# Row convolutions as six products for four pixels on whole images, shorter reciprocal roots, and new due times in a planned kernel

## The chip, the cores and the metric

The kernel runs on one core of one Trainium2 chip. The metric is device time in microseconds (us) of one execution, compared by the median of several. The engines have the profile's names: PE is TensorE (matmuls), PEld its weight loads, DVE is VectorE, ACT is ScalarE, POOL is GpSimd, SP is SyncE, which here only issues transfers.

## The reference

The input is `x`, eight images of 256 channels and 32 x 32 pixels in float32. Four layers follow, each added to its input. Each but for the last sees the input normalised in 32 groups of channels.

```python
x = x + _L0_conv_ref(_gn(x), ...)   # attention, 8 heads of 64, q and k scaled to length one
x = x + _L1_conv_ref(_gn(x), ...)   # 3x3 convolution 256 -> 256, weights times a scale per output channel
x = x + _L2_conv_ref(_gn(x), ...)   # 3x3 convolution 256 -> 256
x = x + _L3_conv_ref(_gn(x), ...)   # mixer: 4 branches of a selective scan, gate, three row filters,
                                    # attention with 8 heads of 32, gelu, 3x3 filter per channel, projection

def _gn(v, G=32, eps=1e-5):
    B_, C_, H_, W_ = v.shape
    g = v.reshape(B_, G, C_ // G, H_, W_)
    m = jnp.mean(g, axis=(2, 3, 4), keepdims=True)
    s = jnp.var(g, axis=(2, 3, 4), keepdims=True)
    return ((g - m) / jnp.sqrt(s + eps)).reshape(v.shape)

def _L2_conv_ref(inp, kernel, bias):
    out = lax.conv_general_dilated(inp, kernel, window_strides=(1, 1), padding=((1, 1), (1, 1)), ...)
    return out + bias[None, :, None, None]
```

The output is the last `x`. The change concerns the two 3x3 convolutions (layers 1 and 2), every reciprocal root of the normalisations, one small product of the mixer's gate, and the order of all work.

## The kernel before

Every operation is first recorded and then put in order by a planner inside the kernel, so that all instructions of the profile carry one line, L252, that of the recorder's call. `gather` joins neighbouring matmuls, `depend` finds what each must wait for, and `rank` gives each group a due time: the work belongs to streams, one per image and part, and the table `PACE` holds seven marks for each stream, between which the due times are laid by the share of the stream's work done. A due time is never earlier than that of what the operation depends on. `arrange` then simulates the engines with a small cost table and issues, on the engine that is free first, the ready group that can start first, by due time among equals. What results is one fixed order per engine. The marks decide nothing but this order.

The streams of an image are A (attention of layer 0), O (its projection), C (both convolutions), N (normalisations ahead of the mixer), F0 to F3 (front of each branch), S (the scans), Z0 to Z3 (end of each branch), B (gate, filters, attention of the mixer) and E (end). W and V prepare weights at the start. Several images are under way at once: while TensorE works at the attention of one image, VectorE runs the scans of another. Only one image can be in C at a time, since the tile `xt` of the pool `xp` has one buffer; so does the tile `taps`.

A convolution (`conv3x3`) works in halves of 16 rows. `transform` normalises the image into `taps` on ScalarE, odd and even pixels apart, and makes from them, for each pair of pixels of a row, four inputs: the row transform by which two outputs of a three-tap filter need four products in place of six. For each half, each block of 128 output channels (`m`) and each of two parts, twelve matmuls of 256 columns fill one PSUM tile `cv` (two buffers) with two products: six matmuls each, for three rows of the filter and two blocks of input channels. `add_products` then adds them on VectorE to the pixels in `xt`, which lie two floats apart. In layer 1 the scale per output channel is applied there, through `col("s1", m)` and `minus_s1`. The weights of the products are made once at the start by `conv_weights` in the tiles `room`, stored in DRAM (`made_w`, 12 pieces of 256 KB for each layer), and loaded by `chunk` from there, piece by piece through ScalarE's queue, for each half again.

`inverse_root` makes a reciprocal root in 11 small operations on VectorE: two for a first guess from the bits, and three Newton steps of three. Four callers use it: `group_stats`, the lengths of q and k, `layer_norm`, and the normalisation in `back_end`, 12 calls an image.

In `back_layers` the gate's 1-wide convolution is one matmul of 128 output columns for each of two blocks and two halves, with the weights spread out in `qpr`.

Of the kernel before, what the change touches and what calls it, by code (L numbers as in the profile page):

```python
# [12 lines left out]
F32 = mybir.dt.float32  # L13
I32 = mybir.dt.int32
AF = mybir.ActivationFunctionType
ALU = mybir.AluOpType
# [23 lines left out]
        (-1169, -859, -431, 125, 565, 748, 863),  # L40
        (2031, 2138, 2230, 2316, 2394, 2427, 2468),
        (3022, 3122, 3226, 3328, 3426, 3535, 3634),
        (4218, 4286, 4354, 4427, 4500, 4575, 4647),
        (5274, 5344, 5414, 5494, 5578, 5649, 5689),
        (6338, 6402, 6470, 6543, 6618, 6719, 6822),
        (7394, 7477, 7560, 7650, 7740, 7826, 7869),
        (8432, 8500, 8566, 8639, 8712, 8760, 8799),
    ),
    "B": (
        (3742, 3818, 3894, 3959, 4024, 4099, 4174),  # L50
        (4850, 4908, 4966, 5025, 5083, 5138, 5192),
        (5827, 5907, 5970, 6049, 6107, 6107, 6280),
        (6819, 6852, 6882, 7048, 7214, 7265, 7312),
        (7970, 8053, 8136, 8225, 8314, 8393, 8472),
        (9010, 9104, 9202, 9300, 9398, 9514, 9630),
        (10029, 10029, 10029, 10122, 10143, 10411, 10586),
        (12739, 12779, 12790, 12925, 12925, 12925, 12925),
    ),
    "C": (
        (1590, 1668, 1685, 1828, 1928, 1928, 1981),  # L60
        (1459, 2140, 2729, 2891, 3004, 3103, 3202),
        (3333, 3631, 3802, 3930, 4058, 4186, 4314),
        (4584, 4720, 4870, 4997, 5122, 5250, 5374),
        (5516, 5743, 5908, 6052, 6195, 6329, 6462),
        (6973, 7034, 7094, 7165, 7233, 7365, 7527),
        (7722, 7896, 8016, 8164, 8316, 8462, 8608),
        (8801, 8855, 9006, 9179, 9350, 9442, 9586),
    ),
    "E": (
        (4173, 4210, 4252, 4314, 4346, 4378, 4412),  # L70
        (5281, 5299, 5322, 5360, 5390, 5426, 5463),
        (6271, 6328, 6375, 6404, 6452, 6489, 6531),
        (7362, 7383, 7418, 7456, 7517, 7539, 7559),
        (8230, 8230, 8477, 8544, 8580, 8609, 8648),
        (9051, 9054, 9067, 9081, 9151, 9151, 9156),
        (10314, 10413, 10427, 10973, 11043, 11080, 11119),
        (10605, 10611, 10611, 10621, 10759, 10804, 10844),
    ),
    "F0": (
        (936, 936, 936, 992, 1236, 1236, 1289),  # L80
        (2142, 2142, 2375, 2438, 2500, 2699, 2699),
        (1749, 1791, 1821, 1868, 1868, 1967, 1995),
        (2036, 2036, 2127, 2174, 2174, 2174, 2174),
        (2752, 2933, 2957, 3038, 3038, 3176, 3176),
        (3833, 3833, 3833, 3880, 3880, 3883, 3883),
        (7322, 7383, 7488, 7535, 7637, 7778, 7778),
        (4815, 4875, 4875, 4922, 4993, 4993, 5007),
    ),
    "F1": (
        (2076, 2151, 2335, 2371, 2411, 2420, 2432),  # L90
        (3681, 3742, 3771, 3771, 3789, 3798, 3807),
        (4629, 4639, 4648, 4671, 4765, 4775, 4784),
        (5763, 5791, 5809, 5840, 5882, 5903, 5940),
        (6643, 6661, 6670, 6716, 6801, 6809, 6892),
        (7897, 7897, 7933, 7950, 7956, 7972, 7980),
        (8743, 8757, 8769, 8817, 8833, 8845, 8851),
        (9880, 9881, 9912, 10075, 10121, 10181, 10225),
    ),
    "F2": (
        (2483, 2632, 2659, 2683, 2686, 2696, 2724),  # L100
        (3391, 3605, 3653, 3712, 3782, 3828, 3866),
        (4779, 4809, 4840, 4849, 4849, 4938, 5017),
        (5860, 5870, 5879, 5899, 5942, 5952, 5965),
        (6960, 6979, 7003, 7004, 7005, 7061, 7143),
        (7482, 7818, 8051, 8054, 8055, 8139, 8147),
        (8917, 9009, 9012, 9027, 9046, 9065, 9128),
        (10350, 10379, 10379, 10492, 10492, 10492, 10492),
    ),
    "F3": (
        (2951, 2953, 2976, 2976, 2996, 2996, 3002),  # L110
        (4074, 4078, 4080, 4081, 4091, 4143, 4210),
        (5062, 5119, 5141, 5146, 5158, 5184, 5247),
        (6098, 6100, 6114, 6114, 6123, 6273, 6386),
        (7109, 7138, 7166, 7203, 7257, 7277, 7353),
        (8377, 8384, 8391, 8432, 8450, 8453, 8500),
        (9289, 9311, 9331, 9331, 9331, 9341, 9408),
        (10811, 10811, 10811, 10815, 10815, 10815, 10815),
    ),
    "N": (
        (-721, -721, -719, -694, -694, -375, -322),  # L120
        (792, 849, 849, 1025, 1763, 1835, 1835),
        (1854, 1854, 1854, 1854, 1854, 1897, 2131),
        (1094, 1117, 1128, 1226, 1226, 4468, 6014),
        (4191, 4193, 4193, 4350, 4350, 4677, 4847),
        (4700, 4700, 4700, 4700, 4700, 4813, 4838),
        (6559, 6654, 6654, 6654, 6654, 6732, 6732),
        (7299, 7299, 7299, 7313, 7313, 7314, 7695),
    ),
    "O": (
        (2052, 2052, 2092, 2101, 2104, 2104, 2109),  # L130
        (2440, 2440, 2442, 2506, 2528, 2619, 2658),
        (3608, 3632, 3649, 3701, 3731, 3752, 3770),
        (4659, 4659, 4704, 4704, 4704, 4704, 4704),
        (5731, 5762, 5778, 5800, 5800, 5811, 5815),
        (6790, 6818, 6831, 6831, 6853, 6853, 6855),
        (7980, 7995, 8002, 8007, 8007, 8012, 8019),
        (8777, 8905, 8909, 8909, 8909, 8919, 8921),
    ),
    "S": (
        (2406, 2724, 2768, 2976, 3146, 3269, 3410),  # L140
        (3494, 3698, 3902, 4034, 4182, 4361, 4540),
        (4529, 4737, 4950, 5093, 5238, 5409, 5573),
        (5564, 5777, 5988, 6129, 6269, 6446, 6622),
        (6667, 6869, 7053, 7214, 7359, 7529, 7696),
        (7697, 7932, 8138, 8275, 8411, 8578, 8763),
        (8777, 8978, 9185, 9338, 9524, 9669, 9853),
        (10860, 10860, 10860, 10869, 10880, 10900, 10900),
    ),
    "V": (
        (-528, -402, -399, 138, 415, 459, 459),  # L150
    ),
    "Z0": (
        (2585, 2611, 2631, 2682, 2705, 2755, 2761),
        (3563, 3649, 3649, 3649, 3649, 3896, 4005),
        (4787, 4787, 4827, 4831, 4878, 4924, 4965),
        (5794, 5794, 5806, 5980, 6230, 6230, 6230),
        (6835, 6842, 6868, 6877, 6877, 7018, 7030),
        (7547, 7547, 7628, 7960, 7983, 8769, 8891),
        (8907, 8957, 8998, 9005, 9013, 9291, 9316),
        (10109, 10118, 10158, 10340, 10340, 10345, 10490),  # L160
    ),
    "Z1": (
        (2375, 2417, 2433, 2705, 2793, 2846, 3222),
        (3815, 3815, 3815, 3845, 3936, 3965, 4022),
        (4921, 4945, 4958, 5048, 5091, 5103, 5133),
        (5915, 5953, 5970, 5970, 6079, 6085, 6088),
        (7089, 7093, 7093, 7095, 7097, 7101, 7135),
        (8059, 8083, 8108, 8113, 8113, 8113, 8363),
# [2209 lines left out]
```

## Time and profile before

| | |
|---|---|
| median of 3 runs | 5131.74 us (5129.71 to 5144.03) |
| the profiled execution | 5126.34 us, its span 5124.6 us |
| TensorE matmul | 4740.6 us busy, 93% of the span, 19178 records |
| VectorE | 4040.2 us busy, 79%, 5586 instructions |
| ScalarE | 2908.5 us busy, 57%, 3829 instructions |
| mean granted clock of TensorE | 0.957 |
| convolution matmuls (`cv<-taps,w`) | 737.5 us busy, 3072 records |
| transfers | 575.20 MB, of them `w<-wc` 384 times 256 KB |

Each float32 matmul leaves two records of weight load and two of matmul. Matmuls of less than 128 rows or columns can run beside each other; the busy time of an engine is the time in which at least one of its instructions runs, and a mean duration of a group can contain overlap with its neighbours. The granted clock is the share of TensorE's full clock that was granted.

### The profile page before, as it was taken

How to read it: one execution, taken by the hardware profiler on the slowest of the kernel's cores; microseconds unless marked ns; L12 is line 12 of the kernel's file. 1: busy time of each engine (PE TensorE's matmuls, PEld its weight loads, DVE VectorE, ACT ScalarE, POOL GpSimd, SP SyncE). 2: the span in 40 equal slices, each digit the busy share in tenths (PEclk: the TensorE clock that was granted, in tenths of full speed). 3: DMA queues.
4: the chain of work that ended last, by engine and by line, in shares of the span. 5: the costliest groups of instructions: out<-in, count | busy, mean ns of one | idle time of the engine just before them, and what ended most of it. 6: DMA issues, size and time to landing. Idle time of an engine off the chain costs nothing.

```text
span 5124.6 us, 53905 instructions
## 1 busy us (share of the span) xinstructions
PE 4740.6 (93%) x19178; PEld 1940.5 (38%) x19178; DVE 4040.2 (79%) x5586; ACT 2908.5 (57%) x3829; POOL 17.8 (0%) x26
## 2 busy tenths in 40 slices
PE   8999799999999999999999999998999899888796
PEld 3362253253432534243442344325343343422323
DVE  4336989996988967988797998788778899799802
ACT  4426545556665565656566566555656557566352
POOL 0000000000000000000000000000000000000000
PEclk9999999999999999999999999999999999899897
DMA  4133253343333433433433353325333344334200
GB/s 135 46 124 113 98 171 120 100 153 116 116 113 102 136 104 113 121 108 125 130 95 104 114 169 112 106 69 162 117 97 112 124 140 152 95 125 125 81 23 25
DMA packets 256662, 575.20 MB, mean 112 GB/s; under 512 B 51192, under 2 KB 79224, under 8 KB 256384
## 3 DMA queue, kind: packets, MB, share of 16 engines
q1 hardware_dynamic: 167680, 431.11, 26.9%
q10 hardware_dynamic: 88704, 140.55, 8.9%
q8 instruction: 154, 2.52, 0.2%
q14 instruction: 124, 1.02, 0.1%
HBM read 483.18 MB, written 63.18 MB: 107 GB/s over the span
## 4 chain that ended last, share of the span: by engine, by line
PE 64%; DVE 24%; ACT 6%; issue 3%; DMA 3%; SPq 1%; DVEq 0%; ACTq 0%
PE big L252 36%; PE cv L252 14%; DVE hs L252 14%; PE acc L252 11%; PE y L252 3%; ACT p L252 2%; DVE room L252 1%; DVE st L252 1%; DVE p L252 1%; DVE u L252 1%; DVE xt L252 1%; DVE xm L252 1%; SPq L252 1%; DVE taps L252 1%; ACT taps L252 1%
## 5 line engine op out<-in xcount | busy, mean ns | idle before, releaser
L252 ACT ACTIVATE p<-big 128x1024 f32<-128x1024 f32 x1024 | 1013.9, 1019 | 555.0 <-PE big L252 489.0
L252 ACT ACTIVATE da<-dt,a_neg 128x512 f32<-128x512 f32 x1024 | 728.1, 720 | 609.2 <-DVE hs L252 494.4
L252 PE MATMUL acc<-p,v 128*64 128x512 f32 x3072 | 833.1, 624 | 41.7 <-ACT p L252 37.4
L252 PE MATMUL cv<-taps,w 128*128 128x256 f32 x3072 | 737.5, 391 | 26.9 <-DVE taps L252 20.7
L252 PEld LDWEIGHTS cv<-taps,w 128*128 128x128 f32 x3072 | 580.0, 193 | 264.7 <-issue 137.0
L252 DVE TENSOR_TENSOR hs<-du,bc 128x1024 f32<-128x1024 f32 x512 | 615.3, 1213 | 64.8 <-PE y L252 55.8
L252 DVE TENSOR_TENSOR hs<-hs,bc 128x1024 f32<-128x1024 f32 x512 | 623.8, 1218 | 31.8 <-ACT carry L252 30.3
L252 DVE TENSOR_TENSOR_SCAN hs<-da,carry,hs 128x512 f32<-128x512 f32 x512 | 637.6, 1273 | 2.1 <-ACT da L252 1.8
L252 PE MATMUL big<-q,k 64*128 64x512 f32 x2048 | 586.7, 652 | 36.4 <-ACT p L252 25.9
L252 DVE TENSOR_TENSOR_SCAN hs<-da,hs 128x512 f32<-128x512 f32 x512 | 608.9, 1213 | 5.6 <-ACT da L252 3.8
L252 DVE TENSOR_TENSOR p<-p 128x1024 f32<-128x1024 f32 x256 | 312.2, 1220 | 205.5 <-ACT p L252 125.9
L252 PEld LDWEIGHTS acc<-p,v 128*64 128x64 f32 x3072 | 161.8, 136 | 603.0 <-issue 416.0
L252 PE MATMUL y<-hs,sel 128*32 128x512 f32 x2048 | 318.5, 632 | 69.6 <-DVE hs L252 61.8
L252 PEld LDWEIGHTS big<-q,k 64*128 64x128 f32 x2048 | 160.9, 188 | 432.6 <-issue 210.8
L252 PE MATMUL big<-qk,qk 32*128 32x512 f32 x2048 | 303.4, 645 | 5.6 <-ACT qk L252 1.6
L252 PE MATMUL cv<-p,v 128*64 128x512 f32 x1024 | 279.1, 612 | 0.0
L252 PE MATMUL big<-xn,w 128*128 128x512 f32 x512 | 236.3, 608 | 6.7 <-ACT big L252 4.1
L252 PE MATMUL big<-o,w 128*128 128x512 f32 x384 | 178.6, 608 | 5.3 <-DVE o L252 2.0
L252 PE MATMUL big<-room,w 128*128 128x512 f32 (+3 forms) x308 | 149.5, 640 | 29.2 <-ACT room L252 27.0
L252 PEld LDWEIGHTS big<-qk,qk 32*128 32x128 f32 x2048 | 84.3, 184 | 193.7 <-issue 140.6
L252 PEld LDWEIGHTS y<-hs,sel 128*32 128x32 f32 x2048 | 48.1, 110 | 272.0 <-DVE hs L252 123.4
L252 DVE TENSOR_TENSOR xt<-xt,cv 128x512 f32<-128x512 f32 (+1 forms) x128 | 69.2, 550 | 102.9 <-PE cv L252 102.4
(235 smaller groups left out, 5114.3 us busy)
## 6 DMA issues: line engine op xcount, KB each, us to landing
bc<-bc SPq DMA_DIRECT2D x256, 512.0 KB
w<-wc ACTq DMA_DIRECT2D x384, 256.0 KB
dt<-dt_m SPq DMA_DIRECT2D x128, 512.0 KB
du<-du_m SPq DMA_DIRECT2D x128, 512.0 KB
rs<-inv SPq DMA_DIRECT2D x64, 256.0 KB
raw<-xm SPq DMA_DIRECT2D x64, 256.0 KB
dt_m<-dt SPq DMA_DIRECT2D x128, 128.0 KB
du_m<-a SPq DMA_DIRECT2D x128, 128.0 KB
```

Of the source, the lines that this page charges most:

```text
L252: made = op["call"](*args, **kwargs).ins
```

## The change

Five things change.

- A row is transformed in fours: six products for four pixels in place of four for two. `taps` has six inputs of 32 x 8, a convolution runs on the whole image and no longer in halves, and the rows above and below the image are no longer zeros in `taps`: the matmuls of the outer filter rows leave the edge row out. There are three parts with two products each.
- The pixels in `xt` now lie four floats apart in each access. In two of the three parts, ScalarE first copies the second product into the place of an input that is no longer needed (`spare`); VectorE makes the difference in PSUM and the sum in that place, and adds both to the pixels with the factors of the transform.
- The scale of layer 1 goes into the weights at the start, by a product with a spread-out column; `conv_weights` makes 18 pieces for each layer.
- `inverse_root` has eight operations: a first guess in one, one step of four and one of three.
- The tables `qpr` and the wide `mean_w` are given up: their matmuls read a column with step zero, and the gate's matmul becomes two of 64 output columns. `PACE` has new marks throughout.

```diff
 PACE = {
...
     "C": (
-        (1590, 1668, 1685, 1828, 1928, 1928, 1981),
-        (1459, 2140, 2729, 2891, 3004, 3103, 3202),
...
+        (650, 761, 761, 795, 795, 795, 795),
+        (229, 1415, 2141, 2216, 2330, 2483, 2528),
...
     "V": (
-        (-528, -402, -399, 138, 415, 459, 459),
+        (-1344, -1191, -383, 287, 1041, 1212, 1445),
     ),
...
-    mean_w = wp.tile([P, P], F32, name="mean_w")
-    pool.memset(mean_w, 1.0 / C)
+    mean = wp.tile([P, 1], F32, name="mean")
+    pool.memset(mean, 1.0 / C)
+    mean_w = mean.to_broadcast([P, P])
...
-    taps = wp.tile([P, 2, 4, 18, 16], F32, name="taps")
+    taps = wp.tile([P, 2, 6, 32, 8], F32, name="taps")
...
     def inverse_root(x):
...
-        vector.tensor_scalar(bits, x.bitcast(I32), 1, None, ALU.logical_shift_right)
         vector.tensor_scalar(
-            y.bitcast(I32), bits, -1.0, float(0x5F3759DF), ALU.mult, ALU.add
+            y.bitcast(I32), x.bitcast(I32), -0.5, float(0x5F3759DF), ALU.mult, ALU.add
         )
-        for last in (False, False, True):
-            vector.tensor_mul(t, y, y)
-            vector.scalar_tensor_tensor(t, t, -0.5, x, ALU.mult, ALU.mult)
-            vector.scalar_tensor_tensor(
-                x if last else y, t, 1.5, y, ALU.add, ALU.mult
-            )
+        vector.tensor_mul(t, y, y)
+        vector.tensor_mul(t, t, x)
+        vector.scalar_tensor_tensor(t, t, -10.0 / 3.0, t, ALU.add, ALU.mult)
+        vector.scalar_tensor_tensor(y, t, 5.0, y, ALU.add, ALU.mult)
+        vector.tensor_mul(t, y, y)
+        vector.scalar_tensor_tensor(t, t, -27.0 / 1024.0, x, ALU.mult, ALU.mult)
+        vector.scalar_tensor_tensor(x, t, 9.0 / 16.0, y, ALU.add, ALU.mult)
...
-    def conv_weights(name):
+    def conv_weights(name, scaled):
         for i in range(6):
+            m, dy = divmod(i, 3)
...
+            if scaled:
+                ps = big_tile()
+                tensor.matmul(
+                    ps[:, 0:P], col("s1", m).to_broadcast([P, P]), ident,
...
+                vector.tensor_copy(by, ps[:, 0:P])
+                w_rows = room[0][:, 0 : 6 * P].rearrange("p (k n) -> p k n", n=P)
+                vector.tensor_mul(
+                    w_rows, w_rows, by.unsqueeze(1).to_broadcast([P, 6, P])
+                )
...
-    def transform(xt, stats, h):
+    def transform(xt, stats):
         scale, shift = stats
...
+        for c in range(2):
+            scalar.activation(
+                taps[:, c, 1:5],
+                xt[c].rearrange("p (h w k) -> p k h w", w=8, k=4),
+                AF.Identity,
+                bias=shift[:, c : c + 1],
+                scale=scale[:, c : c + 1],
+            )
+        t = [taps[:, :, k] for k in range(6)]
+        flat = [a.rearrange("p c h w -> p c (h w)") for a in t]
+        vector.tensor_sub(t[0][:, :, :, 1:8], t[4][:, :, :, 0:7], t[2][:, :, :, 1:8])
+        vector.tensor_sub(t[5][:, :, :, 0:7], t[1][:, :, :, 1:8], t[3][:, :, :, 0:7])
+        for k, src, at in ((0, 2, 0), (5, 3, 7)):
+            scalar.mul(t[k][:, :, :, at], t[src][:, :, :, at], -1.0)
+        vector.tensor_sub(flat[4], flat[4], flat[2])
+        vector.tensor_sub(flat[3], flat[3], flat[1])
+        for to, part, scale, more, op in (
...
+            vector.scalar_tensor_tensor(
+                flat[to], flat[part], scale, flat[more], ALU.mult, op
+            )
...
+    def add_products(x, ps, part, spare):
+        pixels = x.rearrange("p (h w k) -> p k h w", w=8, k=4)
+        products = ps.rearrange("p (k h w) -> p k h w", k=2, w=8)
+        if part == 2:
+            vector.tensor_add(pixels[:, 0:4:3], pixels[:, 0:4:3], products)
+            return
+        a, b = products[:, 0], spare
+        scalar.activation(b, products[:, 1], AF.Copy)
+        vector.tensor_sub(a, a, b)
+        vector.scalar_tensor_tensor(b, b, 2.0, a, ALU.mult, ALU.add)
+        if part == 0:
+            for k, src in ((0, b), (1, a)):
+                to = pixels[:, k:4:2]
+                vector.tensor_add(
+                    to, to, src.unsqueeze(1).to_broadcast([P, 2, 32, 8])
                 )
+            return
+        for k, src, scale in ((0, b, 1.0), (1, a, 2.0), (2, b, 4.0), (3, a, 8.0)):
+            to = pixels[:, k]
+            vector.scalar_tensor_tensor(to, src, scale, to, ALU.mult, ALU.add)
+
+    def conv3x3(xt, mv, made, name, bname, finish):
+        transform(xt, group_stats(mv, cv_tile))
+        for m in range(2):
+            scalar.activation(xt[m], xt[m], AF.Identity, bias=col(bname, m))
+        for part, ks, spare in ((2, (0, 5), None), (0, (1, 2), 0), (1, (3, 4), 5)):
             for m in range(2):
+                ps = cv_tile()
+                w = [chunk(name, 9 * m + 3 * part + dy) for dy in range(3)]
+                for i, k in enumerate(ks):
...
+                    for n in range(6):
+                        dy, c = (1, 0, 2)[n // 2], n % 2
+                        first, last = max(0, 1 - dy), min(32, 33 - dy)
+                        tensor.matmul(
+                            rows[:, first:last],
+                            w[dy][:, 2 * c + i],
+                            taps[:, c, k, first + dy - 1 : last + dy - 1],
+                            start=n == 0,
+                            stop=n == 5,
+                        )
+                add_products(xt[m], ps, part, taps[:, m, spare] if part < 2 else None)
+                if part == 1:
                     channel_stats(made, m, xt[m])
+                    finish(m)
...
-                tensor.matmul(
-                    ps[:, HALVES[h]],
-                    qpr[:, 2 * j : 2 * j + 2].rearrange("q b m -> q (b m)"),
...
+                for b in range(2):
+                    tensor.matmul(
+                        ps[b * DM : (b + 1) * DM, HALVES[h]],
+                        qpw[:, 2 * j + b : 2 * j + b + 1].to_broadcast([96, DM]),
+                        q4[0:96, HALVES[h]],
+                        start=True,
+                        stop=True,
+                    )
```

## The prediction

> **What bounds the kernel now.** I read the page's engine rows first, then busy time by stage, then the same stages for the convolutions' own instructions, then the groups by shape, the chain, and what TensorE waits for.
>
> The page's first rows, and busy time by stage (columns: stretch, length, then busy time and instruction count of PE, PEld, DVE, ACT, POOL, then granted clock, DMA share, GB/s):
>
> ```profile
> span 5124.6 us, 53905 instructions
> ...
> PE 4740.6 (93%) x19178; PEld 1940.5 (38%) x19178; DVE 4040.2 (79%) x5586; ACT 2908.5 (57%) x3829; POOL 17.8 (0%) x26
> ```
>
> ```profile
> 0.00:255.00 255.00, 233.91 (x869) 78.07 (x870) 101.32 (x283) 114.19 (x135) 3.31 (x18) 0.99 0.29 91
> 255.00:510.00 255.00, 240.48 (x993) 123.16 (x993) 129.56 (x245) 116.20 (x159) 0.00 (x0) 0.98 0.38 117
> 510.00:4320.00 3810.00, 3602.95 (x14809) 1489.62 (x14808) 3267.04 (x4408) 2260.48 (x3004) 10.83 (x6) 0.97 0.38 120
> 4320.00:4830.00 510.00, 424.99 (x1610) 152.79 (x1608) 470.14 (x524) 303.16 (x412) 3.61 (x2) 0.90 0.37 111
> 4830.00:5124.60 294.60, 238.23 (x910) 96.86 (x906) 72.14 (x128) 114.48 (x122) 0.00 (x0) 0.88 0.10 31
> ```
>
> There are three regimes. Up to 510 us TensorE leads and VectorE is about half idle. From 510 to 4320 us TensorE is busy 94.6% and VectorE 85.7%: TensorE bounds, VectorE is close behind. From 4320 to 4830 us VectorE leads at 92% (scans of the last image), and the last 295 us are that image's attention and output.
>
> The next lines are the stages again, for the instructions on the tile taps alone (columns as before, without POOL). The convolutions lie in the second and third stage and nowhere behind 4320 us:
>
> ```profile
> 255.00:510.00 255.00, 84.42 (x384) 72.46 (x384) 10.01 (x30) 8.31 (x24) 0.98 0.38 117
> 510.00:4320.00 3810.00, 653.06 (x2688) 507.49 (x2688) 91.14 (x265) 79.38 (x224) 0.97 0.38 120
> ```
>
> Groups by shape (busy us, mean ns): the matmuls of the change, its transform and its drains:
>
> ```profile
> L252 PE MATMUL cv<-taps,w 128*128 128x256 f32 x3072 | 737.5, 391 | 26.9 <-DVE taps L252 20.7 <-issue 3.9 <-DVE xm L252 0.7
> L252 DVE SCALAR_TENSOR_TENSOR xt<-cv,vec,xt 128x512 f32<-128x512 f32 x64 | 47.8, 747 | 69.5 <-PE cv L252 68.8
> L252 DVE TENSOR_TENSOR xt<-xt,cv 128x512 f32<-128x512 f32 x64 | 43.8, 684 | 102.6 <-PE cv L252 102.4
> L252 DVE TENSOR_TENSOR xt<-xt,cv 128x256 f32<-128x256 f32 x64 | 25.4, 416 | 0.4
> L252 DVE SCALAR_TENSOR_TENSOR taps<-taps 128x272 f32<-128x272 f32 x32 | 13.7, 434 | 0.9 <-ACT taps L252 0.6
> L252 DVE TENSOR_TENSOR t<-y 128x2 f32<-128x2 f32 x216 | 33.4, 155 | 3.2
> ```
>
> TensorE waits 20.7 us for taps in the whole run: the transform is hidden now, while VectorE itself waits 102.4 us for the products. One piece of the chain gives the rate of an undisturbed run of convolution matmuls (start, us, what), 218 ns a record:
>
> ```profile
> 344.19 20.96 PE cv L252 x96
> ```
>
> **The change, part by part.**
>
> *Matmuls.* Every float32 matmul leaves two records. A convolution has 2 halves x 2 outputs x 2 parts x 2 products x 6 = 96 matmuls, 192 records of 256 columns; afterwards 3 parts x 2 outputs x 2 products x 6 = 72, 144 records, of which 48 have 256 columns and 96 have 31 rows of 8, 248 columns. Priced by columns that is (48 + 96 x 248/256)/192 = 141/192 of before, so 26.6% of 737.5 us goes: 196 us of busy time (173 us in the third stage, 22 us in the second). At the undisturbed 218 ns it is 51 x 16 x 0.218 = 178 us; if a 248-column record costs as much as one of 256, 48 x 16 x 0.218 = 168 us. I take 196, since the slow stretches of the clock that raise 218 to 240 ns a record stay in proportion. All of it lies on the engine that bounds both stages.
>
> *The gate's products.* A 128-column matmul becomes two of 64 columns, 16 records an image for 8. Eight take 3.68 us now; the attention's 128*64 pairs, which alternate column halves like these, take 1.08 us for four records, so 16 take 4.3 us: +0.6 us an image, +5 us in all. If the halves did not run beside each other (128*64 matmuls that do not alternate: 1.88 us for four), it would be +31 us. I take 5. The mean's weights read with step zero as ln_r's do (weight load 215 ns against 193, beside matmuls): nothing, at most 22 ns on some hundred loads, 3 us.
>
> *VectorE.* Rows of 416 ns at 256 and 684 ns at 512 elements give 1.05 ns an element. Transform: 8 three-operand operations and 2 subtractions of 512, 2 of 448 (618 ns) = 8.1 us a convolution, 129 us in all, against 112 us of taps rows now: +17. Products, per output: 0.684 for the outer pair, 0.416 + 0.417 + 2 x 0.684 for the first inner pair, 0.416 + 0.417 + 4 x 0.417 for the second: 5.39 us, x 32 = 172 us, against 148 us of xt rows: +25. Roots: 96 calls (216/3 of two columns, 24 of eight) lose 3 of 11 operations. At the row's 155 ns that is 45 us; between independent operations such a one delays the next by only 0.07 us (a start at 607.77 and the next at 607.84), then 20 us. I take 33. Net +9 us, between -3 and +22.
>
> *Strides.* One price the trace does not show: the pixels are now touched four floats apart, 16 bytes, where it was 8. An 8-byte stride costs nothing (684 ns, against 685 ns for a plain drain of 512 to mdtw). The only wider strides are ScalarE's edge columns, 222 ns for 16 elements and 221 ns for 17, too short to tell. So the bounds are zero and a doubling of the stride-4 elements: 2 x 2,560 a convolution at 1.05 ns, x 16 = +86 us of VectorE, and 2 x 1,024 at 0.81 ns, +27 us, on ScalarE. I take zero, by the nearest row, and keep 86 for the range. [...]
>
> *ScalarE and queues.* Taps and bias: 140.5 us of rows now, 8.8 us a convolution; afterwards two 1024-wide transforms and two bias passes at 1.23, two edges at about 0.26, four copies of 256 at about 0.37: 6.9 us, -30 us. The weight pieces fall from 384 to 288 of 256 KB, -32 us of issue at 0.33 us on ScalarE's queue, -25 MB. ScalarE is 57% busy, so I cost all this at nothing; uncovered it would be a gain of up to 62 us. SP loses 16 stores of xd.
>
> *Preparation of weights.* Per slice VectorE goes from 1.56 us (0.42 + 0.29 + 2 x 0.425) to 0.42 x 2 + 0.29 x 3 + 0.425 x 4 = 3.4 us, for six slices another 1.2 us for the scaling, four stores on SP in place of three; +29 us of VectorE, and six small matmuls queued in TensorE's order. Cover: preparation ends at 145 us and the first transform starts at 239 us, with VectorE at 40%. I cost it at nothing; had it no cover, up to 29 us.
>
> **The sum**, against the profiled execution, 5126.34 us (span 5124.6). First stage and everything behind 4320 us: 0. Second: -20 of its 22. Third: TensorE's busy time becomes 3603 - 173 + 4 = 3434 us. At today's 94.6% that is 3630 us, -180. But VectorE keeps its 3267 + 8 = 3275 us and would stand at 90%. Both can be full at once: from 2921 to 3049 us TensorE is busy 97% and VectorE 94%. Still, the closer VectorE comes, the more often its queue ends a wait of TensorE. I take one point less of TensorE, 93.5%: 3673 us, -137, VectorE 89.2%. Together -157: 4969, and the median of the three runs stands 5.4 us over the profiled one: 4975 us.
>
> The idle time matters twice: where TensorE is often idle the granted clock falls (0.81 from 576 to 640 us, 1.00 where it is full). [...]
>
> **The rivals.** (1) VectorE takes over: the 16-byte strides cost their full 86 us, 75 in the third stage, so 3350 us there. At the same 89.2% share the stage takes 3756 us: -54 - 20, 5057 us. For: 85.7% already. Against: stride 2 is free. (2) Slower: the transform is now one chain for the whole image, 12 VectorE operations of 8.1 us behind 2.5 us of ScalarE, with a scan operation of 1.2 us possibly before each (14 us); it cannot start on the second half early, and all matmuls wait for it. From 196/16 = 12.2 us of newly exposed wait per convolution it eats the whole gain; at 18 us it gives 5132 + 16 x 18 - 196 = 5224 us. For: in one early transition (627 to 636 us) TensorE already waits 3.9 and 4.7 us. Against: 20.7 us of such waiting in sixteen convolutions. (3) VectorE's share cannot rise at all: 3275/0.857 = 3821 us, and only the 20 us of the second stage remain, 5112 us. (4) TensorE keeps its 94.6% and the new order shortens the end by some 20 us: -222, 4910 us.
>
> **How the numbers follow.** A difference under 0.3% (15 us) cannot be told from none here. My forecast, 4935 to 5015 us: 0.50; (4), down to 4890: 0.14; (1) and what lies between it and the forecast: 0.18; (3): 0.09, a third of it within 15 us; (2): 0.09. The range 4895 to 5060 leaves out (2), (3) and the thin low end. Faster 0.88, same 0.03, slower 0.09.
>
> **What would show it.** Right: 2304 records of cv<-taps,w with some 540 us; taps and xt rows of VectorE near 300 us in all; 288 of the small root operations gone; third stage near 3670 us, VectorE near 89%, clock about 0.97; nothing lost behind the last convolution. Wrong: stride-4 rows of 256 elements well over 420 ns (rival 1); TensorE's waits for taps or xt in the hundreds of us with a clock below 0.95 (rival 2); fewer than 2304 records not saving in proportion.

## The result and the profile after

The changed kernel takes 5154.86 us (median of 6 runs, 5153.85 to 5172.07) against 5133.51 us of the kernel before beside it (5129.71 to 5150.37): a ratio of 1.0043, 95% interval 1.0023 to 1.0063. It is slower by 21 us, where 157 us less were forecast. Its profiled execution has a span of 5153.5 us and a mean granted clock of 0.942 (before 0.957).

The page's engine rows of the kernel after:

```profile
span 5153.5 us, 51809 instructions
...
PE 4619.1 (90%) x18486; PEld 1814.6 (35%) x18486; DVE 4125.4 (80%) x5352; ACT 2906.8 (56%) x3668; POOL 17.6 (0%) x26
```

TensorE's busy time fell by 121.5 us (4740.6 to 4619.1). Its idle time, span less busy, rose by 150.4 us (384.0 to 534.4). The sum, +28.9, is the difference of the two spans. The convolutions' own matmuls fell by more, by 190.8 us (737.5 to 546.7), so all other matmuls together were busy 69 us longer. An estimate from the mean granted clocks, 0.957 and 0.942, with matmul time taken as inverse to them, makes 64 us of that. So matmul time was saved, and more than all of it came back: 150 us as waiting, 69 us as longer matmuls elsewhere.

Busy time by stage (columns as in the prediction):

```profile
0.00:255.00 255.00, 229.29 (x860) 75.93 (x860) 120.99 (x328) 112.05 (x125) 3.19 (x18) 0.98 0.32 101
255.00:510.00 255.00, 241.41 (x972) 112.45 (x976) 147.66 (x237) 128.15 (x161) 0.00 (x0) 0.98 0.36 108
510.00:4320.00 3810.00, 3461.26 (x14036) 1362.00 (x14030) 3292.89 (x4141) 2237.30 (x2830) 10.84 (x6) 0.95 0.37 113
4320.00:4830.00 510.00, 417.79 (x1622) 154.82 (x1619) 467.31 (x513) 305.77 (x422) 3.61 (x2) 0.88 0.37 116
4830.00:5153.50 323.50, 269.40 (x1004) 109.37 (x1002) 96.51 (x139) 123.52 (x133) 0.00 (x0) 0.89 0.11 34
```

The same for instructions on the tile taps alone (the column of POOL is absent):

```profile
255.00:510.00 255.00, 63.37 (x288) 55.72 (x288) 29.14 (x49) 8.12 (x12) 0.98 0.36 108
510.00:4320.00 3810.00, 474.13 (x1980) 378.72 (x1980) 220.08 (x356) 90.20 (x110) 0.95 0.37 113
```

In the third stage TensorE stands at 90.8% (94.6% before), VectorE at 86.4% (85.7%): both near VectorE's old share, and neither near the 93.5% and 89.2% of the sum. The convolutions' own TensorE time in the two stages is 537.5 us and 737.5 before; the last 36 of their 2304 records now lie behind 4320 us. The last convolution matmul starts at 4348.8 us, 29.5 us later than before (4319.3); what follows it takes as long as before. All of the loss therefore lies ahead of it.

Groups by shape in the kernel after (busy us, mean ns | idle before, releaser):

```profile
L252 PE MATMUL cv<-taps,w 128*128 128x248 f32 x1536 | 377.9, 384 | 0.0
L252 PE MATMUL cv<-taps,w 128*128 128x256 f32 x768 | 215.5, 405 | 27.4 <-DVE xt L252 11.5 <-ACT da L252 6.2 <-DVE taps L252 3.3
L252 DVE SCALAR_TENSOR_TENSOR taps<-taps 128x512 f32<-128x512 f32 x128 | 85.5, 679 | 0.8
L252 DVE TENSOR_TENSOR xt<-xt,cv 128x512 f32<-128x512 f32 x64 | 70.6, 1104 | 75.6 <-PE cv L252 75.5
L252 DVE SCALAR_TENSOR_TENSOR xt<-cv,xt 128x256 f32<-128x256 f32 x64 | 40.2, 628 | 0.1
L252 ACT ACTIVATE taps<-xt,norm 128x1024 f32<-128x1024 f32 x32 | 70.0, 2234 | 34.6 <-DMA w<-wc 18.1 <-DVE norm L252 16.4
L252 DVE TENSOR_TENSOR t<-y 128x2 f32<-128x2 f32 x144 | 21.6, 154 | 2.0
```

There are 2304 records of convolution matmuls, as forecast; the two shapes together are busy 546.7 us, their overlap counted once. Operations within taps cost 679 ns for 512, as forecast. What touches the pixels in `xt` does not: 1104 ns where 684 was taken, 628 where 417 was taken, and 2234 on ScalarE where 1.23 us was.

The chain that ended last, by engine and by line: first the kernel before, then after.

```profile
PE 64%; DVE 24%; ACT 6%; issue 3%; DMA 3%; SPq 1%; DVEq 0%; ACTq 0%
```

```profile
PE 56%; DVE 28%; ACT 9%; issue 4%; DMA 2%; SPq 0%; ACTq 0%; DVEq 0%
PE big L252 34%; DVE hs L252 16%; PE acc L252 10%; PE cv L252 9%; ACT p L252 3%; PE y L252 2%; DVE xt L252 2%; DVE p L252 1%; DVE room L252 1%; ACT taps L252 1%; DVE st L252 1%; DVE taps L252 1%; DVE u L252 1%; ACT da L252 1%; DVE xm L252 1%
```

TensorE had only 64% of the chain before, at a busy share of 93%: the path went through VectorE or ScalarE for 30% of the time, whatever TensorE did meanwhile. That line stood on the page before and was not used for the sum. Alone it would have taken off only a part: 64/93 is 0.69, and 0.69 of the 196 us is still 135 us (an estimate). The loss is densest between 510 and 1030 us: 31 of the 150 us of new idle time lie in these 520 us (53.8 us before, 85.1 after). The largest of TensorE's waits there, before and then after (total us, times, longest):

```profile
PE y L252 <- DVE hs L252: 18.1, 6, 4.7
```

```profile
PE y L252 <- DVE hs L252: 27.3, 10, 6.9
PE big L252 <- ACT p L252: 11.1, 6, 4.2
PE big L252 <- DVE mv L252: 7.1, 1, 7.1
```

One such place, TensorE alone (start, us, what, in brackets the idle time and its releaser), with busy time by engine for the same stretch:

```profile
601.30 1.92 PE L252 MATMUL y<-hs,sel 128*32 128x512 f32 x4 [6.87 <-DVE hs L252]
607.52 1.92 PE L252 MATMUL y<-hs,sel 128*32 128x512 f32 x4 [4.30 <-DVE hs L252]
612.70 1.92 PE L252 MATMUL y<-hs,sel 128*32 128x512 f32 x4 [3.25 <-DVE hs L252]
```

```profile
593.00:626.00 33.00, 18.20 (x62) 10.77 (x63) 31.58 (x37) 17.11 (x24) 0.00 (x0) 0.69 0.30 105
```

VectorE is nearly full there (31.6 of 33 us), alternating scan operations with the transform's, TensorE is busy 18 of 33 us, with waits of 6.9, 4.3 and 3.3 us, and the granted clock is 0.69. The four records behind each of these waits take 1.92 us; the four at 593.38 us, behind a wait of 0.49 us, take 1.05 us.

### The profile page after: what moved, and what is told of

The parts are those of the page before. It is cut to its first block, busy times and chain, and to the rows that moved or that the text cites. A ratio compares the mean times of both kernels' runs of the same rounds, so it can differ in the third digit from the quotient of the medians.

```text
span 5153.5 us, 51809 instructions
## 1 busy us (share of the span) xinstructions
PE 4619.1 (90%) x18486; PEld 1814.6 (35%) x18486; DVE 4125.4 (80%) x5352; ACT 2906.8 (56%) x3668; POOL 17.6 (0%) x26
## 4 chain that ended last, share of the span: by engine, by line
PE 56%; DVE 28%; ACT 9%; issue 4%; DMA 2%; SPq 0%; ACTq 0%; DVEq 0%
PE big L252 34%; DVE hs L252 16%; PE acc L252 10%; PE cv L252 9%; ACT p L252 3%; PE y L252 2%; DVE xt L252 2%; DVE p L252 1%; DVE room L252 1%; ACT taps L252 1%; DVE st L252 1%; DVE taps L252 1%; DVE u L252 1%; ACT da L252 1%; DVE xm L252 1%
## 5 line engine op out<-in xcount | busy, mean ns | idle before, releaser
L252 PE MATMUL cv<-taps,w 128*128 128x248 f32 (+1 forms) x2304 | 546.7, 391 | 27.4 <-DVE xt L252 11.5
L252 PEld LDWEIGHTS cv<-taps,w 128*128 128x128 f32 x2304 | 440.8, 196 | 195.4 <-issue 97.1
L252 PEld LDWEIGHTS big<-qk,qk 32*128 32x128 f32 x2048 | 86.4, 186 | 210.4 <-issue 157.1
L252 PEld LDWEIGHTS big<-xn,w 128*128 128x128 f32 x512 | 95.6, 192 | 135.6 <-issue 114.2
```

Source lines behind the costliest of these rows:

```text
L252: made = op["call"](*args, **kwargs).ins
```

## The experiments

In all kernels but five the order of every engine is that of the kernel they start from: the planner sees all operations, and those marked are left out only when the order is issued. The five others (both exchanges of marks, both with shaken marks, one of the whole versions) are planned anew. Ratios are to the kernel before, run beside each. Where two changed kernels are compared in us, the difference of their medians and that of their ratios can differ by up to 8 us; both are given where it matters. A kernel with something left out does not compute the reference's values; it serves for its time alone.

**1. Strides.** The pixels are touched in runs of eight floats where they were four floats apart; the same instructions, in the same order. The columns of an image are then permuted in the convolutions.

```diff
-xt[c].rearrange("p (h w k) -> p k h w", w=8, k=4)      # transform
+xt[c].rearrange("p (h k w) -> p k h w", w=8, k=4)
-x.rearrange("p (h w k) -> p k h w", w=8, k=4)          # add_products
+x.rearrange("p (h k w) -> p k h w", w=8, k=4)
```

> The kernel after, each engine's order of instructions unchanged, but the four pixel planes of a row are taken as four runs of eight neighbouring floats instead of every fourth float (the columns of a row are permuted by that, so the values are not the convolution's). This takes away the 16-byte strides alone. Theory A (the strides' price took the gain): ScalarE's transform falls from 2234 to about 1234 ns, VectorE's 512-wide drains from 1104 to about 684 ns and the 256-wide ones from 630 to about 417 ns, 69 us of VectorE and 32 us of ScalarE less, and most of it shows: 5155 falls to 5060 to 5090 us. Theory B (the marks and the order they give are what holds the kernel, whatever the engines' work): the rows fall the same way, but the time stays within 25 us, 5130 to 5155 us.

Measured: 5093.12 us, ratio 0.992 [0.9902, 0.9938]. Against the kernel after that is 62 us by the medians, 63 by the ratios. Its engine rows, and those of the strides:

```profile
PE 4599.5 (90%) x18486; PEld 1809.9 (36%) x18486; DVE 4060.7 (80%) x5352; ACT 2874.1 (57%) x3668; POOL 17.6 (0%) x26
```

```profile
L252 DVE TENSOR_TENSOR xt<-xt,cv 128x512 f32<-128x512 f32 x64 | 43.2, 675 | 75.5 <-PE cv L252 75.5
L252 ACT ACTIVATE taps<-xt,norm 128x1024 f32<-128x1024 f32 x32 | 38.0, 1233 | 34.6 <-DVE norm L252 34.5
L252 DVE SCALAR_TENSOR_TENSOR xt<-cv,xt 128x256 f32<-128x256 f32 x64 | 26.4, 413 | 0.1
```

The stride alone had raised 675 to 1104, 413 to 628 and 1233 to 2234 ns. It is the difference between slower and faster than before.

**2. Which strides.** The runs of eight in `add_products` alone (the second pair of lines above); `transform` as in the change.

> The kernel after, order kept, with VectorE's products (the drains) alone written and read as runs of eight floats; the transform on ScalarE and VectorE keeps its 16-byte strides. The pixels' order then differs between the two, so the values are not the reference's. Theory A (VectorE's strides in the drains made the loss): most of the 62 us that runs of eight brought come back, 5095 to 5115 us. Theory B (the 32 us on ScalarE, in a chain for which all matmuls of a convolution wait, count as much as they last): 5125 to 5140 us.

Measured: 5129.31 us, ratio 0.9979 [0.9969, 0.9989]. VectorE's row is short again, ScalarE's is not:

```profile
L252 ACT ACTIVATE taps<-xt,norm 128x1024 f32<-128x1024 f32 x32 | 70.0, 2235 | 34.6 <-DVE norm L252 34.6
L252 DVE TENSOR_TENSOR xt<-xt,cv 128x512 f32<-128x512 f32 x64 | 43.3, 676 | 75.3 <-PE cv L252 75.3
```

VectorE's 62 us (4125.4 to 4063.6 us busy) bring 26 us by the medians, 33 by the ratios; the other 36 or 30 come with ScalarE's 32 us. So the transform's strides count in full or nearly so, on an engine that is 56% busy, and the drains' strides for about half. What waits for ScalarE's pass is VectorE's part of the transform: its first subtractions wait 43.8 us for taps in this run and 17.1 us in experiment 1 (first line here, second there). How that reaches the end of the run is not shown; TensorE itself waits for taps only some 3 us in either.

```profile
L252 DVE TENSOR_TENSOR taps<-taps 128x448 f32<-128x448 f32 x32 | 19.3, 622 | 43.8 <-ACT taps L252 43.8
L252 DVE TENSOR_TENSOR taps<-taps 128x448 f32<-128x448 f32 x32 | 19.2, 620 | 17.1 <-ACT taps L252 17.1
```

**3. What TensorE's time is worth in the old order.** In the kernel before, 3 of the 12 convolution matmuls of each PSUM tile are left out, nearly the change's saving.

```diff
 dy, c = divmod(n, 2)
+plan.left_out = n == 1 or (n == 3 and i == 0)
```

> The kernel before, its order kept, with a quarter of the convolution matmuls left out at issue (three of twelve of each PSUM tile), so that TensorE loses about as much as the change takes from it and nothing else changes. If TensorE is the bound that the prediction took it for, 184 us of busy time go and the time falls by 130 to 180 us, to 4955 to 5005 us. If the order with VectorE behind it holds the pace (theory B), under 60 us are seen: 5075 to 5130 us, with TensorE's busy share falling and its granted clock lower.

Measured: 5064.23 us, ratio 0.986 [0.9839, 0.9881], 72 us for 184 us of nominal matmul time, or 0.39. The convolution row falls by 164 us (737.5 to 573.3), TensorE's busy time by 121 us, since the other matmuls take 43 us more (granted clock 0.951, before 0.957), and TensorE's idle time rises by 61 us:

```profile
PE 4619.3 (91%) x18410; PEld 1806.1 (36%) x18410; DVE 4035.8 (80%) x5586; ACT 2903.7 (57%) x3829; POOL 17.7 (0%) x26
```

```profile
L252 PE MATMUL cv<-taps,w 128*128 128x256 f32 x2304 | 573.3, 396 | 41.0 <-DVE taps L252 17.0 <-issue 11.2 <-DVE xt L252 6.6
```

Nothing else was changed here, neither other operations nor order. The step "all of it lies on the engine that bounds both stages" fails on this run alone.

**4. The same in the new order.** In the kernel after, half of the convolution matmuls are left out (n in 1, 2, 4 of six), half of 546.7 us.

> The kernel after, its order kept, with half of the convolution matmuls left out at issue (about 270 us of TensorE's busy time). If TensorE still bounds it, the time falls by 150 to 230 us, below 5000 us. If after the change TensorE's time is no longer what counts, under 60 us: above 5095 us.

Measured: 5116.56 us, ratio 0.9956 [0.9938, 0.9975]: 38 us by the medians, 45 by the ratios, for 273 us of nominal matmul time. In the new order a matmul left out is worth still less.

**5. The transform as the new wait** (the slower rival). In the kernel after, 6 of the transform's 8 three-operand operations are left out, 64 us of VectorE.

```diff
+plan.left_out = (to, part) in ((2, 2), (1, 1), (0, 0), (5, 3))
 vector.scalar_tensor_tensor(flat[to], flat[part], scale, flat[more], ALU.mult, op)
```

> The kernel after, its order kept, with six of the eight three-operand operations of each transform left out at issue: 64 us of VectorE less, and each convolution's matmuls can start some 4 us of operations, and the scan operations between them, earlier. If the long transform is what TensorE waits for (the second rival of the prediction), the time falls by more than the 64 us, to 5050 us or less. If it is only VectorE's work that counts, by 40 to 64 us, 5090 to 5115 us. If neither, under 20 us.

Measured: 5143.06 us, ratio 1.001 [0.9999, 1.0021], 12 us by the medians, 17 by the ratios. These operations of the transform's chain cost a little; they did not eat the gain. The chain's part on ScalarE is that of experiment 2.

**6. Drains and roots.** First, in the kernel of experiment 1, the last four operations of each output's products are left out (the `for k, src, scale` loop of `add_products`). Second, in the kernel before, one Newton step of three is left out (`plan.left_out = step == 1`).

> The kernel after with runs of eight (5093 us), order kept, with the last four operations of each output's products left out (128 of 415 ns, 53 us of VectorE between the last matmul of a convolution and its statistics). The pixels lose the products of one pair. Theory A (the longer drains are what the changed kernel without strides still pays, 25 us): 20 to 45 us faster, 5050 to 5075 us. Theory B (hidden, like the transform): within 12 us, 5080 to 5105 us.

> The kernel before, order kept, with one of three Newton steps of the reciprocal roots left out (3 operations in each of 96 calls, 288 in all, which is how many operations the change's eight-operation root saves). Prediction's term: 33 us of VectorE. If a root lies on the chain (statistics, then the normalisation that TensorE waits for), 15 to 40 us faster, 5095 to 5120 us. If VectorE's time does not count here, as with the sums left out: within 10 us, 5123 to 5135 us.

Measured: 5095.9 us, ratio 0.9911 [0.989, 0.9933], against 0.992 with them in: nothing that can be told from zero. And 5128.31 us, ratio 0.9986 [0.9974, 0.9997]: 7 us for 288 operations, where 33 us of VectorE was the term. As VectorE's busy time the term was right: it falls by 31.8 us (4040.2 to 4008.4).

**7. VectorE's time in the old order.** Every second sum of the attention's p is left out, alone and together with experiment 3's matmuls.

```diff
-total = pair["sums"][-1]
+total, plan.left_out = pair["sums"][-1], kt % 4 == 3
```

> The kernel before, its order kept, with half of the additions of attention weights in layer 0 left out at issue (128 of 1.22 us, 156 us of VectorE, on tiles that nothing of the convolutions uses). If TensorE alone bounds the kernel before, as the prediction read the stages, the time falls by less than 30 us. If VectorE holds the pace beside it, by 60 to 120 us: 5015 to 5075 us.

> The kernel before, every engine's order kept, with both cuts at once: 3 of 12 convolution matmuls per PSUM tile (about 184 us of TensorE, alone worth 71 us) and every second sum of the attention's p (156 us of VectorE, alone worth 5 us). Theory A (the two engines take turns in setting the end, so that each cut alone is caught by the other engine): together clearly more than 71 + 5, 110 to 200 us faster, 4935 to 5025 us. Theory B (what remains is waits in a fixed order, at other places than these two): the gains add, 65 to 90 us faster, 5045 to 5070 us.

Measured: 5129.07 us, ratio 0.9989 [0.9979, 1.0], 6 us at most for 156 us of VectorE, and hardly to be told from zero. Together 5055.89 us, ratio 0.9837 [0.9821, 0.9853], 84 us: the sum of the two within their intervals. So these sums neither bound the kernel nor caught TensorE's saving.

**8. The scan's part of VectorE.** Every second product of scan states and bc is left out, 312 us of VectorE: in the kernel before, there with experiment 3's matmuls, and in experiment 1's kernel.

```diff
+plan.left_out = u["gp"] == 1
 vector.tensor_mul(hs, hs, both_groups(u["bc"][:, 1]))
```

> The kernel before, every engine's order kept, with every second product of scan states and bc (hs<-hs,bc) left out: 256 of 1.218 us, 312 us of VectorE. Theory A (the scan's operations on VectorE are the other side of the path, hs has 14% of the chain for 2486 us of busy time, a share of 0.29): 50 to 110 us faster, 5025 to 5085 us. Theory B (VectorE's time does not count in this order wherever it is, as with the attention's sums): within 15 us, 5120 to 5140 us.

> Both cuts at once, order kept: the 256 products of the scan states (312 us of VectorE) and the quarter of the convolution matmuls (184 us of TensorE, alone 71 us). Theory A (the scan's VectorE work is what caught the saved TensorE time): more than the sum of the two, the matmuls now worth 100 us or more on top of the products. Theory B (the gains add): the matmuls worth 60 to 80 us on top of the products.

> The kernel after with runs of eight (5093 us), order kept, with the same 256 products of scan states left out. Between 510 and 1030 us hs has 34.9% of this kernel's chain, against 20.6% before. Theory A (in the new order the scan's VectorE work bounds more of the time): it gains clearly more than the kernel before gains from the same cut, 100 to 180 us, 4915 to 4995 us. Theory B (the new order depends on it no more than the old): the same gain as in the kernel before, within 20 us.

Measured: 5089.41 us, ratio 0.9906 [0.9887, 0.9924], 48 us, a share of 0.15 where 0.29 was read off the chain: the chain's share overstates here too what a saving is worth. With the matmuls 4996.78 us, ratio 0.9727 [0.9709, 0.9746], 140 us: on top of the products the matmuls are worth 92 us, not 72, between the two theories' figures. In the new order 5052.54 us, ratio 0.9825 [0.9802, 0.9848], less than experiment 1's kernel by 41 us (medians) or 49 (ratios): the same as in the old, within the intervals. The chain by engine of the first, kernel before with half the products left out:

```profile
PE 74%; DVE 12%; ACT 7%; DMA 4%; issue 3%; SPq 1%; ACTq 0%; DVEq 0%
```

So the scan may catch a part of what TensorE saves: some 20 us, out of three ratios with intervals of about 10 us each. The changed kernel does not depend on the scan more than the old one did.

**9. The marks.** The kernel before with the change's `PACE`, the kernel after with the old `PACE`, and both with every mark moved at random by at most 3 units.

> The kernel before with the change's marks in PACE and nothing else, so that the planner orders the old convolutions by the new due times. If the new marks are poor in themselves, the time rises by much: 5200 us or more, and with them the change would have been carried down. If marks matter little, it stays within 30 us of 5134 us. If the new marks are better ones, below 5100 us.

> The kernel after with the marks of before in PACE and nothing else. If the marks set anew are what lost the gain (theory B), the old ones do as well or better: 5100 us or less. If the new marks were fitted to the new convolutions and helped them, the old ones are slower: 5190 us or more. If marks matter little, within 30 us of 5155 us.

> The kernel after with every mark of PACE moved at random by at most 3 units (the marks run from -1368 to some 8000), the order planned anew with them; the same operations and shapes. Theory A (the order is fitted to its exact marks, so that a few units decide tens of us): over 30 us from the kernel after, most likely slower, 5185 to 5350 us. Theory B (the order's quality is a smooth matter of the marks): within 20 us of the kernel after, 5135 to 5175 us.

> The kernel before with every mark of PACE moved at random by at most 3 units, the order planned anew with them; the same operations and shapes. Theory A (fitted to its exact marks): over 30 us slower, 5165 to 5350 us. Theory B (smooth): within 20 us, 5115 to 5155 us.

Measured: exchanged 5468.41 us, ratio 1.0651 [1.0629, 1.0672], and 5326.13 us, ratio 1.0373 [1.0353, 1.0394]. Shaken: the kernel after 5291.36 us, ratio 1.0302 [1.0277, 1.0328], the kernel before 5377.1 us, ratio 1.0467 [1.0442, 1.0492]. With one random draw each, moves of at most three units cost 136 and 239 us, with the same operations and shapes. The marks run from -4116 to 12925 before and from -6336 to 12710 after; -1368 to some 8000, as the expectation has it, are those of stream A alone. The page of the kernel before with shaken marks:

```profile
span 5374.4 us, 53977 instructions
...
PE 4812.3 (90%) x19178; PEld 1953.6 (36%) x19178; DVE 4040.4 (75%) x5586; ACT 2916.9 (54%) x3830; POOL 17.8 (0%) x26
```

VectorE's busy time is what it was (4040.2). The order alone can move the time of this kernel by as much as the 157 us that the change's work was to save.

**10. A version that keeps both gains.** The runs of eight with the reference's output: the input is laid out in runs of eight before the launch, which the device time does not contain (layer 0 does not depend on the order of pixels), and two ScalarE copies per block of channels put the last convolution's pixels back, through places of taps that are free by then, ahead of the store of `xd`. Once all operations were planned anew; once the change's own order was kept and the copies set in just ahead of each store.

```diff
-sync.dma_start(out=img["xd"][:, m], in_=xt[m])
+row = taps[:, :, 3 * m : 3 * m + 2].rearrange("p c k h w -> p c (k h w)")
+for h in range(2):
+    scalar.activation(
+        row[:, h].rearrange("p (h w k) -> p h k w", w=8, k=4),
+        xt[m][:, HALVES[h]].rearrange("p (h k w) -> p h k w", w=8, k=4), AF.Copy)
+sync.dma_start(out=img["xd"][:, m].rearrange("p (c n) -> p c n", c=2), in_=row)
```

> The change with the layout of the first experiment throughout: the pixels of a row of x lie as four runs of eight from the start (the attention of layer 0 does not mind the order of its tokens), and two copies of ScalarE per block put them back in order behind the second convolution, 64 more operations of 512 elements, 40 to 70 us of ScalarE in all with 16-byte strides on one side. By theory A this keeps most of what the layout gave: 5090 to 5115 us, faster than both kernels. If the planner's order, which changes with the added operations, matters more than that, anything from 5070 to 5170 us.

> The kernel after with pixels kept in runs of eight through the convolutions (x is laid out so by its loads; two ScalarE copies of 512 for each half of a convolution's last output put them back in natural order ahead of its store), and with the change's own order of all other operations; the reference is computed. 64 copies of about 0.8 us are new on ScalarE, 51 us of an engine that is 56% busy. Theory A (the order kept, copies hidden for the most part): 5090 to 5120 us, faster than before and after. Theory B (any operation added to a fitted order costs as the planned anew version did): above 5150 us.

Measured: planned anew 5334.18 us, ratio 1.0388 [1.0371, 1.0405]. In the change's order 5103.38 us, ratio 0.9927 [0.9913, 0.994]: 0.7% faster than before and about 1% faster than after. There are 32 copies, not 64 as the expectations counted (only the last convolution of an image stores), and they take 33.1 us:

```profile
L255 ACT ACTIVATE taps<-xt 128x512 f32<-128x512 f32 x32 | 33.1, 1141 | 17.7 <-DVE xt L255 14.6 <-DMA xd<-taps 3.0
```

## Why the prediction was wrong, by its steps

The step that failed is "All of it lies on the engine that bounds both stages", and with it the 93.5% of TensorE in the sum. TensorE was busy 94.6% in the third stage but had 64% of the whole chain, and with the order kept, its time was worth 0.39 of what was left out (experiment 3). The 196 us would then be worth 77 us (an estimate, 0.39 x 196), not the 157 of the sum. A high busy share under a fixed order was no bound: in experiment 3, with nothing else changed, the saving came back in part as 61 us of idle time, spread over many small waits, and as 43 us of longer matmuls elsewhere.

The second failure is a term's size. The strides were taken at zero. They measured 69 us of busy time in VectorE's four rows (the upper bound was 86) and 32 us on ScalarE (27), and 62 us of the kernel's time. The choice "by the nearest row" took a stride of 8 bytes for near to 16, and the rows are not alike: 684 ns for 512 elements at 8 bytes, 1104 ns at 16. The doubling behind the 86 and the 27 was the author's estimate, which no row of before shows; measured, VectorE's rows of 512 and 256 elements became 1.64 and 1.52 times as long, and ScalarE's price lies above its 27.

Together, in us against the kernel before: matmuls -77, strides +62, roots -7, the transform's 17 us of VectorE some +3 (at experiment 5's 12 of 64), drains 0: -19, an estimate. Measured +22 by the ratio, so some 40 us are left. Experiment 1, from which the +62 comes, must leave as many: its kernel saves 41 us where -77, -7 and +3 make 81. A second sight of them is that its TensorE is idle 39 us more than experiment 3's at about the same busy time (484.6 against 445.5 us, spans of 5084.1 and 5064.8). By kind, most of that stands in two waits, of acc for p (attention) and of y for hs (scans): +27 and +9 us, while the others nearly cancel. The rows before, in experiment 3, in experiment 1 and after:

```profile
L252 PE MATMUL acc<-p,v 128*64 128x512 f32 x3072 | 833.1, 624 | 41.7 <-ACT p L252 37.4 <-ACT o L252 0.4 <-ACT both L252 0.3
L252 PE MATMUL y<-hs,sel 128*32 128x512 f32 x2048 | 318.5, 632 | 69.6 <-DVE hs L252 61.8 <-DVE u L252 7.5
```

```profile
L252 PE MATMUL acc<-p,v 128*64 128x512 f32 x3072 | 830.9, 623 | 42.2 <-ACT p L252 37.5 <-ACT o L252 0.4 <-ACT both L252 0.3
L252 PE MATMUL y<-hs,sel 128*32 128x512 f32 x2048 | 324.7, 633 | 75.0 <-DVE hs L252 67.7 <-DVE u L252 6.9
```

```profile
L252 PE MATMUL acc<-p,v 128*64 128x512 f32 x3072 | 836.0, 625 | 69.6 <-ACT p L252 64.3 <-ACT o L252 0.8
L252 PE MATMUL y<-hs,sel 128*32 128x512 f32 x2048 | 319.6, 627 | 82.9 <-DVE hs L252 76.9 <-DVE u L252 3.3 <-DVE t L252 2.5
```

```profile
L252 PE MATMUL acc<-p,v 128*64 128x512 f32 x3072 | 843.0, 630 | 76.0 <-ACT p L252 70.8 <-ACT o L252 0.8
L252 PE MATMUL y<-hs,sel 128*32 128x512 f32 x2048 | 323.4, 629 | 91.1 <-DVE hs L252 85.2 <-DVE u L252 3.3 <-DVE t L252 2.5
```

In the old order these two waits hardly grow when a quarter of the convolution matmuls goes; they grow where the order is new. The transform's operations on VectorE, the last drains, the roots and the scan do not hold the 40 us (experiments 5, 6 and 8), nor does the longer preparation of weights: up to 510 us TensorE is idle 39.3 us, before 35.6. The new order is what remains, and single draws of an order differ by 136 us and more. But that it holds the 40 us is not shown, and at which place stays open, since no run kept the old order with the new convolutions.

Of the rivals, the first (VectorE by strides, 5057) had the right price of the strides on the wrong worth of the matmuls. The third (VectorE's share cannot rise, 5112) came nearest on the shares, 86.4% against 85.7%, but its cause does not hold: in the kernel before, 156 us less of VectorE brought 6, and another 312 brought 48. (Its own division, 3821 us for a stage of 3810, leaves out 11 us and should have given 5123.) The second, the only one on the slower side, named matmuls that wait for the transform: TensorE's wait for taps fell from 20.7 to 3.3 us, and most of the three-operand operations of the transform were worth 12 to 17 us (experiment 5); only its ScalarE pass, through the strides, counted in full. The sign was missed because of the strides: without them the same order is faster than before (experiment 1). None priced a loss by the order itself: the new due times were counted as free or, in the fourth rival, as a gain.

Right were the counts and durations of what was visible: 2304 records (546.7 us busy against some 540), the transform's VectorE operations (126 us against 129), 288 operations fewer in the roots, and nothing lost behind the last convolution. The gate's product cost nothing (38.9 us in its row against 39.3), where +5 was taken. A clock of 0.97 was expected in the third stage and 0.95 was granted. Of the signs of being wrong, rows with a stride of four floats well over 420 ns came true (628), and so did a clock below 0.95 over the run (0.942), without the long waits for taps or xt that were to come with it.

## What to carry to other kernels

Before a saving on the busiest engine is multiplied by its busy share, hold that share against the engine's part of the chain: 93% against 64% was the warning here. It gave no price: the chain's share would have made 0.69 of the saving, and 0.39 was measured. In a kernel with a planned order, leave operations out at issue with the order kept to find what a saving is worth, and keep the order when one is added; a plan made anew can move the time by several times the effect in question. Price a stride by a row with that stride, or keep the upper bound in the sum: here 8 bytes cost nothing (684 ns for 512, against 685 for a plain drain), and 16 bytes made VectorE's rows half as long again or more (413 to 628 ns, 675 to 1104). Lay data out so that neighbours stay neighbours: here that was worth 62 us.

## What the hardware showed that was not expected

- A stride of four floats costs VectorE 0.84 ns more for each element where one of two inputs and the output have it (675 to 1104 ns for 512, 413 to 628 for 256), beside a rate of 1.05 ns without it (416 to 684 ns from 256 to 512 elements in the kernel before). A stride of two floats cost nothing that shows (684 ns for 512, against 685 for a plain drain and 675 in runs of eight).
- On ScalarE it costs 0.98 ns an element when reading (1233 to 2234 ns for 1024) and about as much when writing (0.8 to 1.1 ns, an estimate from rows that differ in more than the stride): the copy of 512 that writes four floats apart takes 1141 ns, copies of 512 out of PSUM 584 ns in the kernel after (`rs<-big`), and a pass of 512 within SBUF 712 ns in the kernel before (`xt<-xt,vec`).
